# Triangle update and Fourier layer on one core: weights prepared on ScalarE in the gathering stage, rows spread by transfers, transposes ahead of the norm's factor, centering in two PSUM tiles

## The chip, the cores and the metric

The kernel runs on one core of one Trainium2 chip. The metric is device time in microseconds (us), the median of several executions. Lower is better. TensorE is written PE, VectorE DVE, ScalarE ACT, GpSimd POOL and SyncE SP; a DMA that SP or POOL issues stands in that engine's queue and starts when the engine's instruction stream reaches it.

## The reference, cut to what matters

The input `x` is 512 x 512 positions with 64 channels, float32. Layer 0 adds a triangle update, layer 1 adds a layer of 12 x 12 Fourier modes. Each is applied to a group norm over the whole image (32 groups of two channels).

```python
x = x + _L0_conv_ref(_gn(x), sequence_mask, norm_w, norm_b, left_w, left_b, ...)
x = x + _L1_conv_ref(_gn(x), w_real, w_imag)

def _L0_conv_ref(x, ...):
    xn = _ln(x, norm_w, norm_b)                      # over the 64 channels
    left  = (xn @ left_w  + left_b)  * mask * sigmoid(xn @ lgate_w + lgate_b)
    right = (xn @ right_w + right_b) * mask * sigmoid(xn @ rgate_w + rgate_b)
    out_gate = sigmoid(xn @ ogate_w + ogate_b)
    out = einsum('bkjd,bkid->bijd', left, right)
    return (_ln(out, onorm_w, onorm_b) @ out_w + out_b) * out_gate
```

`mask` is 1 only where row and column are both in the sequence mask (0 or 1 for each of the 512 rows), so the sides are needed only for masked rows and columns.

## The kernel before, in words

**The path.** The kernel ranks the masked rows first (lines 66 to 137) and, when there are at most K = 256 of them, takes the path `compact`, which this run takes. `slot_t` holds, row by row, the mask and the Fourier basis in rank order; `slot_row` holds each column's place among the masked ones.

**Stage 1, gathering (lines 682 to 725).** `load_weights` (line 685) issues 28 small loads on SP's queue: norm weights, the four weight matrices `raw_sides`, `raw_gates`, `raw_ogate`, `raw_out` and their biases. It returns `makers`, which later makes the steps that fold the norm into each weight: `begin` scales the raw matrix by the norm's weight on DVE (line 177) and multiplies by the centering matrix on PE (lines 179 and 180); `end` copies the result out of PSUM and adds the bias on DVE (lines 186 and 187). Then 16 blocks of 32 columns follow (`jc`, line 703). POOL gathers four tiles of 128 rows per block (line 644), 1 MB each: two with the masked rows (`xg`, two buffers of two tiles) and two with the others (`yg`). PE transposes each (line 713) into `x_ps` (six PSUM tiles), DVE takes the statistics from there (line 714). ACT copies 22 of the 32 columns of `xg` to their slots in `xc`, and POOL the other 10 (line 699, `keep`); since all of these write `xc` at places known only at run time, ACT's and POOL's copies take turns. After its copies POOL issues the gathers of block `jc + 2`. After the last block `group_norm_affine` (line 725) turns the statistics into `ab1`, the scale and shift of each channel: a chain of small DVE instructions with two PE averages (lines 261 to 290).

**Stage 2, sides and gates (lines 729 to 877).** `xc` is worked in 64 groups `q` of four columns. The order on each engine is the written one (`manual_schedule`), a software pipeline from q = -14 to 63 in which one pass of the loop does, for different groups:

- `project(q, "gates")` on PE, then the two sigmoids on ACT (line 839);
- `normed(q + 1)` on DVE (line 786), which reads `rbc`, the layer norm's factors spread over the channels;
- up to three of the nine steps of `rsqrt_steps` on DVE (`todo`);
- `channels(q + 14)`: four PE transposes into `xc_ps` (line 746, two tiles) and one ACT instruction that applies `ab1` (line 747);
- `spread(k)`, each fourth pass: a PE transpose into `rc_ps` (line 771), an ACT copy, then POOL writes the factors to DRAM (`rs_d`, line 775) and reads them back spread, twice 512 KB (`rbc`, line 779);
- one step of `making`, in passes -13 to -6 (line 849): the eight steps of the weights;
- `early`, six prefetches on POOL between q = 11 and 37;
- one step of `prepare`, in passes 51 to 60 (line 853);
- `centered(q + 13)`: four matmuls into the single tile `cc_ps` (line 754) and ACT's squares (line 758), which DVE sums (line 867);
- `project(q, "sides")` on PE, the product of side and gate on DVE (`o_c`, line 862), and two stores of 256 KB from SP's queue (`left_d`, `right_d`, line 874).

The factors of groups 4k to 4k + 3 are spread in pass 4k - 6, and `normed(4k)` runs in pass 4k - 1. `prepare` has ten steps: `mask_of` twice (lines 810 to 813: copy a mask column wide on DVE, transpose it on PE, copy it back on DVE) and `own_of` twice (lines 817 and 818), for the masks `mask_s` and `mask_own` of stage 3; `row_of` twice (lines 799 to 806), the biases of `ogate` and `out` as rows; `indices` twice (lines 822 to 824); and `center_x` and `gate_x` (lines 828 and 829).

**Stage 3 and after.** Stage 3 (from line 882) loads `left_d` and `right_d` channel by channel, multiplies them and applies the masks; its first load waits for the last store of stage 2. Then come output gate, second norm, Fourier layer and output, up to the end.

PSUM is full in stage 2: `xc_ps` two banks, `cc_ps` and `rc_ps` one each, `gates_c0`, `gates_c1`, `sides_c0`, `sides_c1` one each.

Of the kernel before, what the change touches and what calls it, by code (L numbers as in the profile page):

```python
# [46 lines left out]
def conv_preact_kernel(ctx: ExitStack, tc: tile.TileContext, t: dict):  # L47
# [94 lines left out]
    def load_weights(pool, queue):  # L142
# [27 lines left out]

        def steps(keep, room, slots=None):

            made = {}

            def begin(name, nw, nb, raw, b, k):
                scaled = pool.tile([P, P], F32, name="scaled_" + name, tag="scaled")
                nc.vector.tensor_scalar(scaled, raw, nw, None, ALU.mult)
                ps = made[name] = room()
                nc.tensor.matmul(ps[:, :P], center, scaled, start=True, stop=True)
                nc.tensor.matmul(ps[:, P : P + 1], raw[:k], nb[:k], start=True, stop=True)  # L180

            def end(name, nw, nb, raw, b, k):
                ps = made.pop(name)
                weights[name] = raw if slots and name in ("sides", "gates") else keep.tile([P, P], F32, name="w_" + name)
# [6 lines left out]
        return steps  # L191

# [57 lines left out]

    def group_norm_affine(keep, sets, each, name, with_mean=lambda: None, with_variance=lambda ab: None):

# [3 lines left out]
        ab = keep.tile([P, 3], F32, name="ab_" + name)  # L256
        with tc.tile_pool(name="gn_" + name, bufs=1) as gp, tc.tile_pool(
            name="gnp_" + name, bufs=1, space=PSUM
        ) as gps:
            part = gp.tile([P, groups], F32, name="part")  # L260
            nc.vector.tensor_reduce(part, sets[0], AX.X, ALU.add)
            mean_ps = gps.tile([P, groups], F32, name="mean_ps")
            nc.tensor.matmul(mean_ps, avg, part, start=True, stop=True)
# [10 lines left out]
            nc.vector.tensor_reduce(v, d, AX.X, ALU.add)  # L274
            var_ps = gps.tile([P, groups], F32, name="var_ps")
            nc.tensor.matmul(var_ps, avg, v, start=True, stop=True)
# [90 lines left out]
    def general(gc):  # L367
# [10 lines left out]
        with tc.tile_pool(name="wprep", bufs=1) as wp, tc.tile_pool(name="wps", bufs=2, space=PSUM) as wps:  # L378
            for step in load_weights(wp, nc.scalar)(gc, lambda: wps.tile([P, P + 1], F32, name="made_ps")):
                step()  # L380
# [246 lines left out]
    def compact(fc):  # L627
# [53 lines left out]
        with tc.tile_pool(name="wt", bufs=1) as cp:  # L681
            with tc.tile_pool(name="f1", bufs=1) as sp, tc.tile_pool(name="f1x", bufs=2) as xp, tc.tile_pool(
                name="f1y", bufs=4
            ) as yp, tc.tile_pool(name="f1p", bufs=6, space=PSUM) as pt, tc.manual_schedule():
                makers = load_weights(cp, nc.sync)
                sets = chunk_sets(fc, 4, 1)
# [16 lines left out]
                for jc in range(NJ):  # L703
                    if jc % quarter == 0:
                        stats = sp.tile([P, 1, 16 * quarter, 6], F32, name="stats1c")
                    for r in range(4):
                        flat = xgs[jc][1][r].rearrange("p j c -> p (j c)")
                        for c in range(4):

                            ps = pt.tile([P, 4, P], F32, name="x_ps")  # L710
                            for i in range(4):
                                o = (8 * c + 2 * i) * C
                                nc.tensor.transpose(ps[:, i, :], flat[:, o : o + P], ident)  # L713
                            nc.vector.bn_stats(  # L714
                                stats[:, 0, 16 * (jc % quarter) + 4 * r + c, :], ps.rearrange("p i k -> p (i k)")
                            )
                    keep(mybir.EngineType.Activation, nc.scalar.copy, jc, 0, SHARE)
                    keep(mybir.EngineType.Pool, nc.gpsimd.tensor_copy, jc, SHARE, JC)
                    del xgs[jc]
                    if jc + 2 < NJ:  # L720
                        fetch_tile(jc + 2)
                    if jc % quarter == quarter - 1:
                        join_chunks(sp, sets, jc // quarter, stats)

                ab1 = group_norm_affine(fc, sets, 2 * stats.shape[2], "xc")


            rs_d = dram.tile([K // 4, 2, 4 * P], F32, name="rs_d")
            with tc.tile_pool(name="fn", bufs=2) as np_, tc.tile_pool(name="fw", bufs=2) as wk, tc.tile_pool(
                name="fr", bufs=3  # L730
            ) as rp, tc.tile_pool(name="fg", bufs=1) as sp, tc.tile_pool(name="fo", bufs=5) as op, tc.tile_pool(
                name="fpt", bufs=2, space=PSUM
            ) as pt, tc.tile_pool(name="fpc", bufs=1, space=PSUM) as pc, tc.tile_pool(
                name="fpp", bufs=1, space=PSUM
            ) as pp, tc.manual_schedule():
                groups = K // 4
# [5 lines left out]

                def channels(q):
                    tps = pt.tile([P, 4, P], F32, name="xc_ps")
                    for i in range(4):
                        nc.tensor.transpose(tps[:, i, :], xc[:, 4 * q + i].rearrange("p r c -> p (r c)"), ident)
                    nc.scalar.activation(
                        gts(q), tps.rearrange("p i k -> p (i k)"), AF.Identity, bias=ab1[:, 1:2], scale=ab1[:, 0:1]
                    )

                def centered(q):
                    cps = pc.tile([P, 8, C], F32, name="cc_ps")
                    for i in range(4):
# [14 lines left out]
                def spread(k):  # L768

                    ps = pc.tile([QB * 8, P], F32, name="rc_ps")  # L770
                    nc.tensor.transpose(ps, rss.pop(k), ident)
# [23 lines left out]

                def row_of(name):

                    wide = sp.tile([P, P], F32, name="wide_" + name, tag="wide")
                    nc.vector.tensor_copy(wide, biases[name].to_broadcast([P, P]))
                    ps = pt.tile([P, 4, P], F32, name="xc_ps")[:, 0, :C]  # L800
                    nc.tensor.matmul(ps, wide, ident[:, :C], start=True, stop=True)
                    rows_of[name] = fc.tile([P, C], F32, name="bias_row_" + name)
                    nc.vector.tensor_copy(rows_of[name], ps)
                    if name == "out":
                        for r in range(2):
                            nc.sync.dma_start(u_d[:, K, r, :], rows_of["out"])

                def mask_of(b):
                    wide = sp.tile([P, P], F32, name=f"wide{b}", tag="wide")
                    nc.vector.tensor_copy(wide, slot_t[:, b, 1:2].to_broadcast([P, P]))  # L810
                    ps = pt.tile([P, 4, P], F32, name="xc_ps")[:, 0]
                    nc.tensor.matmul(ps, wide, ident, start=True, stop=True)
                    nc.vector.tensor_copy(mask_s[:, b * P : (b + 1) * P], ps)

                def own_of(b):
                    own = sp.tile([P, P], F32, name=f"own{b}", tag="wide")
                    nc.vector.tensor_mul(own, mask_s.rearrange("p (q b) -> p b q", b=2)[:, b], ident)
                    nc.vector.tensor_reduce(mask_own[:, b : b + 1], own, AX.X, ALU.add)

                def indices(b):  # L820
# [738 lines left out]
```

## Time and profile before

| | |
|---|---|
| timed, median of 3 | 1777.51 us (1775.67 to 1780.51) |
| the profiled execution | 1774.54 us |
| its span, first to last instruction | 1772.8 us |
| mean granted PE clock | 0.895 |
| stage 1 | 0 to 195 us |
| norm's factor, to the first ACT instruction of stage 2 | 195 to 201 us |
| stage 2 before the first `normed` | 201 to 232 us |
| stage 2, steady and end | 232 to 447 us |
| stage 3 | 450 to 613 us |

The profile has one row for each instruction or group of instructions: start, duration, engine, line, operation, what is written and read, and in square brackets how long the engine was idle just before and what ended that. `x4` is a count, and then the duration is that of the group. `PEld` is PE's load of the stationary operand. A table by stretches gives each engine's busy time in a window, the clock granted to PE (1.00 is full), the share of time in which the DMA engines were busy, and what they moved.

### The profile page before, as it was taken

What the parts mean: (1) busy time and instruction counts of PE and PEld (TensorE: products, weight loads), DVE (VectorE), ACT (ScalarE), POOL (GpSimd) and SP (SyncE); (2) the same over time, 40 slices, a digit from 0 to 9 for tenths busy, and PEclk for the clock granted to TensorE, in tenths of its full rate; (3) what the DMA queues carried; (4) which work ended last, traced back from release to release, by engine and by line L of the source; (5) the groups of instructions that cost most, each with busy time, mean ns of one, the idle gap of its engine ahead of it and who ended that gap; (6) DMA issues with size and microseconds to landing.
All of it is one profiled execution on the core that took longest, in us unless ns stands there. A gap on an engine that the chain in (4) does not pass through costs nothing. (4 is left out here: it accounts for less than half of the span.)

```text
span 1772.8 us, 32732 instructions
## 1 busy us (share of the span) xinstructions
PE 1559.8 (88%) x10918; PEld 1241.0 (70%) x10918; DVE 1411.4 (80%) x2985; ACT 946.9 (53%) x1724; POOL 935.4 (53%) x693
## 2 busy tenths in 40 slices
PE   6777699998899977999999999999999877998772
PEld 5666566664799866888888988888888744665441
DVE  6989678888455558889999999999999984865551
ACT  3555577774333356777777777777777642011000
POOL 4666111110000027799999999999999881111110
PEclk9999999999999989999999999999999975555555
DMA  7999268987899879568777767776777699999999
GB/s 284 386 380 382 109 174 276 288 276 237 278 309 306 273 217 342 221 203 308 246 257 260 243 237 250 261 254 233 257 264 243 208 305 418 422 426 427 427 427 382
DMA packets 192818, 518.48 MB, mean 292 GB/s; under 512 B 37920, under 2 KB 104736, under 8 KB 151680
## 3 DMA queue, kind: packets, MB, share of 16 engines
q1 hardware_dynamic: 156400, 295.72, 47.5%
q0 software_dynamic: 32768, 218.38, 33.6%
q10 hardware_dynamic: 3472, 2.20, 0.5%
q8 instruction: 88, 1.44, 0.3%
q14 instruction: 90, 0.74, 0.1%
HBM read 311.60 MB, written 204.60 MB: 291 GB/s over the span
## 5 line engine op out<-in xcount | busy, mean ns | idle before, releaser
L1070 PE MATMUL w_ps<-gate_x,xt_c 128*128 128x128 f32 x2048 | 281.1, 281 | 31.3 <-DVE z_t L1299 27.8
L1138 POOL TENSOR_TENSOR xc<-xc,z_t 128x1024 f32<-128x1024 f32 x127 | 301.2, 2372 | 8.1
L1070 PEld LDWEIGHTS w_ps<-gate_x,xt_c 128*128 128x128 f32 x2048 | 252.4, 194 | 48.4 <-DVE z_t L1299 44.2
L1070 PE MATMUL c_ps<-center_x,xt_c 128*128 128x128 f32 x2048 | 277.0, 279 | 1.3 <-ACT xt_c L1104 0.6
L1070 PEld LDWEIGHTS c_ps<-center_x,xt_c 128*128 128x128 f32 x2048 | 252.9, 194 | 4.2 <-ACT xt_c L1065 2.7
L1465 PE MATMUL l_ps<-xc,rinv 24*128 24x512 f32 x512 | 208.2, 1136 | 28.3 <-DVE xc L1472 18.6
L1193 DVE BATCH_NORM_STATS2 stats2c<-xc 128x6 f32<-128x128 f32 x1024 | 220.4, 278 | 8.9 <-POOL xc L1138 8.9
L1108 DVE TENSOR_REDUCE scratch<-sq_c 128x16 f32<-128x1024 f32 x160 | 194.5, 1216 | 24.1 <-ACT sq_c L1103 19.8
L1246 ACT ACTIVATE z_t<-z_t 128x1024 f32<-128x1024 f32 x128 | 135.5, 1059 | 132.8 <-DVE z_t L1305 110.7
L1303 POOL TENSOR_TENSOR z_t<-z_t,bias_row_out 128x1024 f32<-128x1024 f32 x32 | 75.5, 2360 | 245.6 <-DMA xc<-tri_d 223.0
L1465 PEld LDWEIGHTS l_ps<-xc,rinv 24*128 24x128 f32 x512 | 121.2, 306 | 110.5 <-DVE xc L1472 57.1
L1065 ACT ACTIVATE xt_c<-t_ps,ab_xc 128x512 f32<-128x512 f32 x256 | 176.1, 688 | 8.7 <-PE t_ps L1063 7.8
L1299 DVE TENSOR_TENSOR z_t<-w_ps,rs_n 128x512 f32<-128x512 f32 x256 | 172.1, 672 | 6.2 <-PE w_ps L1070 6.1
L714 DVE BATCH_NORM_STATS2 stats1c<-x_ps 128x6 f32<-128x512 f32 x256 | 155.5, 679 | 16.9 <-PE x_ps L713 16.0
L1101 ACT ACTIVATE sq_c<-c_ps 128x512 f32<-128x512 f32 x256 | 150.7, 589 | 31.1 <-PE c_ps L1070 30.6
L1305 DVE TENSOR_TENSOR z_t<-z_t,scratch 128x1024 f32<-128x1024 f32 x128 | 156.3, 1221 | 10.1 <-ACT rs_n L1114 3.5
L1134 POOL TENSOR_TENSOR z_t<-z_t,xc 128x1024 f32<-128x1024 f32 x64 | 151.8, 2371 | 15.7 <-ACT z_t L1246 15.6
L1063 PE MATMUL t_ps<-c_ident,xc 128*128 128x128 f32 x1024 | 157.9, 277 | 0.0
L1472 DVE TENSOR_TENSOR xc<-xc,l_ps 128x512 f32<-128x512 f32 x176 | 109.2, 682 | 56.6 <-DMA xc<-x_h,dst_i 44.4
L1063 PEld LDWEIGHTS t_ps<-c_ident,xc 128*128 128x128 f32 x1024 | 118.0, 142 | 50.9 <-issue 49.8
L1134 POOL TENSOR_TENSOR z_t<-z_t,bias_row_out 128x1024 f32<-128x1024 f32 x63 | 149.4, 2371 | 7.3 <-ACT z_t L1246 6.8
L699 ACT COPY xc<-xg 128x128 f32 x352 | 105.0, 298 | 67.6 <-POOL xc L699 28.7
(212 smaller groups left out, 2563.6 us busy)
## 6 DMA issues: line engine op xcount, KB each, us to landing
x_h<-xc SPq DMA_DIRECT2D x64, 1024.0 KB
out_x<-xc SPq DMA_DIRECT2D x44, 1024.0 KB
xc<-u_d SPq DMA_DIRECT2D x512, 64.0 KB
out_x<-lx_t SPq DMA_DIRECT2D x20, 1024.0 KB
rbc<-rs_d POOLq DMA_DIRECT2D x32, 512.0 KB, 7.0
left_d<-o_c SPq DMA_DIRECT2D x64, 256.0 KB
right_d<-o_c SPq DMA_DIRECT2D x64, 256.0 KB
left_raw<-left_d SPq DMA_DIRECT2D x64, 256.0 KB
```

What stands on the lines that cost most here:

```text
L714: nc.vector.bn_stats(stats[:, 0, 16 * (jc % quarter) + 4 * r + c, :], ps.rearrange("p i k -> p (i k)"))
L1063: nc.tensor.transpose(tps[:, i, :], flat[:, o : o + P], ident)
L1065: nc.scalar.activation(xts[s], tps, AF.Identity, bias=ab1[:, 2:3])
L1070: nc.tensor.matmul(ps[:, 2 * i : 2 * i + 2, :], xts[s][:, i, :], w, start=True, stop=True)
L1101: nc.scalar.activation(sq, cps, AF.Square)
L1108: nc.vector.tensor_reduce(totals[k % 2][:, 8 * (n - 1) : 8 * (n + 1)], sqs.pop(s // 2), AX.X, ALU.add)
L1134: nc.gpsimd.tensor_mul(zs[k, c], zs[k, c], u)
L1138: nc.gpsimd.tensor_add(xr, xr, zs.pop((k, c)))
L1193: nc.vector.bn_stats(st[k // 4][:, g, k % 4, :], x_of(k)[:, :, 2 * g : 2 * g + 2])
L1299: nc.vector.tensor_mul(z[:, 8 * odd : 8 * odd + 8, :], wps, rs)
L1305: nc.vector.tensor_add(z, z, bias_ps["ogate"].unsqueeze(1).to_broadcast([P, 16, C]))
L1465: nc.tensor.matmul(ps.rearrange("p j o -> p (j o)"), rinv[h, b, :], it[h], start=True, stop=True, tile_position=(32 * g, 0),)
```

## The change

The four weights are made in stage 1: ACT scales them before its copies of blocks 5 to 8 (`scale_weights`), PE centers them after the transposes of the same blocks (`center_weights`, into two PSUM tiles of their own, the bias added by a matmul with the identity), and ACT copies them out before its copies of block 10 (`keep_weights`). The masks and the two bias rows no longer go through DVE and PE: SP writes them to DRAM (`m_d`, `b_d`) and reads them back spread. The three mask transfers stand on SP's queue ahead of the weight loads; the bias rows follow `keep_weights`. `group_norm_affine` moves into stage 2's pools and calls `turn_x` for groups 0 to 5 between its second PE average and its `rsqrt`; groups 2 to 5 borrow the PSUM tiles of gates and sides. `centered` alternates, for groups below 13, between `cc_ps` and another tile (`rc_ps`, then tiles of gates and sides). What is left of `prepare` runs in passes 0 to 3 in place of 51 to 60.

```diff
+m_d = dram.tile([K], F32, name="m_d")
+nc.sync.dma_start(m_d.rearrange("(b p) -> p b", p=P), slot_t[:, : K // P, 1])
+nc.sync.dma_start(mask_s, m_d.unsqueeze(0).to_broadcast([P, K]))
+nc.sync.dma_start(mask_own, m_d.rearrange("(p b) -> p b", b=2))
-makers = load_weights(cp, nc.sync)
+loaded, _ = load_weights(cp, nc.sync)
+made = mk.tile([P, 4, P], F32, name="made_w")
+made_b = mk.tile([P, 4], F32, name="made_b")
+def scale_weights(i):
+    name, nw, nb, raw, b, k = loaded[i]
+    scales[i] = cp.tile([P, P], F32, name="scaled_" + name, tag="scaled")
+    nc.scalar.mul(scales[i], raw, nw)
+def center_weights(i):
+    name, nw, nb, raw, b, k = loaded[i]
+    nc.tensor.matmul(made[:, i, :], center, scales.pop(i), start=True, stop=True)
+    nc.tensor.matmul(made_b[:, i : i + 1], raw[:k], nb[:k], start=True, stop=False)
+    nc.tensor.matmul(made_b[:, i : i + 1], ident, b, start=False, stop=True)
+def keep_weights():
+    for i, (name, nw, nb, raw, b, k) in enumerate(loaded):
+        weights[name] = raw if i < 2 else fc.tile([P, P], F32, name="w_" + name)
+        nc.scalar.copy(weights[name], made[:, i, :])
+        biases[name] = b_all[:, i : i + 1]
+    nc.scalar.copy(b_all, made_b)
+    mkp.close()
+    b_d = dram.tile([2, C], F32, name="b_d")
+    for i, name in enumerate(("ogate", "out")):
+        nc.sync.dma_start(b_d[i].rearrange("(c o) -> c o", o=1), biases[name][:C])
+        rows_of[name] = fc.tile([P, C], F32, name="bias_row_" + name)
+        nc.sync.dma_start(rows_of[name], b_d[i].unsqueeze(0).to_broadcast([P, C]))
+    for r in range(2):
+        nc.sync.dma_start(u_d[:, K, r, :], rows_of["out"])
...
 for jc in range(NJ):
+    if 0 <= jc - 5 < 4:
+        scale_weights(jc - 5)
+    if jc == 10:
+        keep_weights()
...
+    if 0 <= jc - 5 < 4:
+        center_weights(jc - 5)
     keep(mybir.EngineType.Activation, nc.scalar.copy, jc, 0, SHARE)
...
-ab1 = group_norm_affine(fc, sets, 2 * stats.shape[2], "xc")
...
+four = ("gates_c0", "gates_c1", "sides_c0", "sides_c1")
+def turn_x(q):
+    if q < 2 or q > 5:
+        tps = pt.tile([P, 4, P], F32, name="xc_ps")
+    else:
+        tps = pp.tile([P, N], F32, name=four[q - 2]).rearrange("p (i k) -> p i k", i=4)
     for i in range(4):
         nc.tensor.transpose(tps[:, i, :], xc[:, 4 * q + i].rearrange("p r c -> p (r c)"), ident)
+    turned_x[q] = tps
 def channels(q):
-    tps = pt.tile([P, 4, P], F32, name="xc_ps")
+    if q not in turned_x:
+        turn_x(q)
+    tps = turned_x.pop(q)
...
 def centered(q):
-    cps = pc.tile([P, 8, C], F32, name="cc_ps")
+    if q % 2 == 0 or q >= lead:
+        cps = spare("cc_ps")
+    else:
+        cps = spare("rc_ps") if q < 7 else pp.tile([P, N], F32, name=four[(q - 7) // 2])
...
-prepare = [lambda b=b: mask_of(b) for b in range(2)] + [lambda b=b: own_of(b) for b in range(2)]
-prepare += [lambda: row_of("ogate"), lambda: row_of("out"), lambda: indices(0), lambda: indices(2)]
+prepare = [lambda: indices(0), lambda: indices(2)]
 prepare += [lambda: nc.vector.tensor_scalar(center_x, center, ab1[:, 0:1], None, ALU.mult)]
 prepare += [lambda: nc.vector.tensor_scalar(gate_x, weights["ogate"], ab1[:, 0:1], None, ALU.mult)]
-making = makers(fc, lambda: pp.tile([P, N], F32, name="gates_c0"), True)
+ab1 = group_norm_affine(
+    fc, sets, 2 * stats.shape[2], "xc", with_variance=lambda ab: [turn_x(q) for q in range(6)],
+    rooms=[lambda k=k: spare(k)[:, :1] for k in ("cc_ps", "rc_ps")],
+)
 for q in range(-lead - 1, groups):
...
-    if q + lead in range(1, 1 + len(making)):
-        making[q + lead - 1]()
...
-    if 0 <= q - (groups - lead) < len(prepare):
-        prepare[q - (groups - lead)]()
+    if 0 <= q < len(prepare):
+        prepare[q]()
```

`mask_of`, `own_of` and `row_of` are gone. Elsewhere the diff only passes these pieces through (`group_norm_affine` takes `rooms`, the pools of `cc_ps` and of the four tiles change places).

More of the change, by code (lines that the diff above doesn't have):

```diff
@@ L169, in load_weights, with steps @@
             loaded.append((name, *norms[norm], raw, b, C if split else P))
-        def steps(keep, room, slots=None):
+        def steps(keep, room):
             made = {}
@@ L183, in end @@
                 ps = made.pop(name)
-                weights[name] = raw if slots and name in ("sides", "gates") else keep.tile([P, P], F32, name="w_" + name)
+                weights[name] = keep.tile([P, P], F32, name="w_" + name)
                 biases[name] = keep.tile([P, 1], F32, name="b_" + name)
@@ L189, in steps @@
             return [lambda part=part, one=one: part(*one) for one in loaded for part in (begin, end)]
-        return steps
+        return loaded, steps
     def rsqrt(pool, total, scale, eps, shape, y=None):
@@ L249, in join_chunks, with group_norm_affine @@
         nc.vector.scalar_tensor_tensor(var, var, 1.0 / count, between, ALU.mult, ALU.add)
-    def group_norm_affine(keep, sets, each, name, with_mean=lambda: None, with_variance=lambda ab: None):
+    def group_norm_affine(keep, sets, each, name, with_mean=lambda: None, with_variance=lambda ab: None, rooms=None):
         groups, n = sets[0].shape[1:]
@@ L256, in group_norm_affine @@
         ab = keep.tile([P, 3], F32, name="ab_" + name)
-        with tc.tile_pool(name="gn_" + name, bufs=1) as gp, tc.tile_pool(
-            name="gnp_" + name, bufs=1, space=PSUM
-        ) as gps:
+        with tc.tile_pool(name="gn_" + name, bufs=1) as gp, ExitStack() as own:
+            if rooms is None:
+                gps = own.enter_context(tc.tile_pool(name="gnp_" + name, bufs=1, space=PSUM))
+                rooms = [lambda k=k: gps.tile([P, groups], F32, name=k + "_ps") for k in ("mean", "var")]
             part = gp.tile([P, groups], F32, name="part")
             nc.vector.tensor_reduce(part, sets[0], AX.X, ALU.add)
-            mean_ps = gps.tile([P, groups], F32, name="mean_ps")
+            mean_ps = rooms[0]()
             nc.tensor.matmul(mean_ps, avg, part, start=True, stop=True)
@@ L274, in group_norm_affine @@
             nc.vector.tensor_reduce(v, d, AX.X, ALU.add)
-            var_ps = gps.tile([P, groups], F32, name="var_ps")
+            var_ps = rooms[1]()
             nc.tensor.matmul(var_ps, avg, v, start=True, stop=True)
@@ L378, in general @@
         with tc.tile_pool(name="wprep", bufs=1) as wp, tc.tile_pool(name="wps", bufs=2, space=PSUM) as wps:
-            for step in load_weights(wp, nc.scalar)(gc, lambda: wps.tile([P, P + 1], F32, name="made_ps")):
+            for step in load_weights(wp, nc.scalar)[1](gc, lambda: wps.tile([P, P + 1], F32, name="made_ps")):
                 step()
@@ new lines, in compact @@
+                mkp = ExitStack()
+                mk = mkp.enter_context(tc.tile_pool(name="mk", bufs=1, space=PSUM))
+                made = mk.tile([P, 4, P], F32, name="made_w")
+                made_b = mk.tile([P, 4], F32, name="made_b")
+                b_all = fc.tile([P, 4], F32, name="b_all")
+                scales = {}
+                def scale_weights(i):
+                    name, nw, nb, raw, b, k = loaded[i]
+                    scales[i] = cp.tile([P, P], F32, name="scaled_" + name, tag="scaled")
+                    nc.scalar.mul(scales[i], raw, nw)
@@ L732, in compact @@
                 name="fpt", bufs=2, space=PSUM
-            ) as pt, tc.tile_pool(name="fpc", bufs=1, space=PSUM) as pc, tc.tile_pool(
-                name="fpp", bufs=1, space=PSUM
-            ) as pp, tc.manual_schedule():
+            ) as pt, tc.tile_pool(name="fpp", bufs=1, space=PSUM) as pp, tc.tile_pool(
+                name="fpc", bufs=1, space=PSUM
+            ) as pc, tc.manual_schedule():
                 groups = K // 4
@@ L741, in gts, with spare, channels @@
                     return xc[:, 4 * q : 4 * q + 4].rearrange("p i r c -> p (i r c)")
-                def channels(q):
-                    tps = pt.tile([P, 4, P], F32, name="xc_ps")
+                four = ("gates_c0", "gates_c1", "sides_c0", "sides_c1")
+                turned_x = {}
+                def turn_x(q):
[3 more added lines that the diff above has]
+                        tps = pp.tile([P, N], F32, name=four[q - 2]).rearrange("p (i k) -> p i k", i=4)
                     for i in range(4):
                         nc.tensor.transpose(tps[:, i, :], xc[:, 4 * q + i].rearrange("p r c -> p (r c)"), ident)
+                    turned_x[q] = tps
+                def spare(name):
+                    return pc.tile([P, N], F32, name=name)
+                def channels(q):
+                    if q not in turned_x:
+                        turn_x(q)
+                    tps = turned_x.pop(q)
                     nc.scalar.activation(
@@ L751, in centered @@
                 def centered(q):
-                    cps = pc.tile([P, 8, C], F32, name="cc_ps")
+                    if q % 2 == 0 or q >= lead:
+                        cps = spare("cc_ps")
+                    else:
+                        cps = spare("rc_ps") if q < 7 else pp.tile([P, N], F32, name=four[(q - 7) // 2])
+                    cps = cps.rearrange("p (i c) -> p i c", c=C)
                     for i in range(4):
@@ L768, in spread @@
                 def spread(k):
-                    ps = pc.tile([QB * 8, P], F32, name="rc_ps")
+                    ps = spare("rc_ps")[: QB * 8, :P]
                     nc.tensor.transpose(ps, rss.pop(k), ident)
@@ L793, in project @@
                     return made
[L796 to L818, printed above, removed]
                 def indices(b):
```

## The prediction

> **What bounds the kernel now.** I read the page's 40 slices first (the clock and DMA rows dip near 200 us and near 410 us), then the table by stretches around both dips, then the timeline inside them, then the waits. Columns of the table: PE, PEld, DVE, ACT and POOL busy, granted PE clock, DMA share, GB/s.
>
> ```profile
> 198.20:201.90 3.70, 2.40 (x11) 2.00 (x11) 1.79 (x12) 0.83 (x2) 0.00 (x0) 0.50 0.02 4
> 201.90:205.70 3.80, 2.94 (x13) 2.54 (x13) 0.88 (x2) 1.99 (x3) 0.00 (x0) 0.59 0.00 0
> 205.70:220.00 14.30, 10.66 (x79) 9.20 (x80) 5.49 (x18) 6.34 (x10) 0.00 (x0) 1.00 0.00 0
> 250.00:400.00 150.00, 150.00 (x891) 91.60 (x887) 129.64 (x273) 110.89 (x187) 26.35 (x39) 1.00 0.89 274
> 404.00:448.00 44.00, 34.81 (x133) 16.46 (x130) 34.98 (x75) 19.53 (x32) 3.50 (x6) 0.96 0.81 246
> ```
>
> From 250 to 400 us PE is busy all the time and the DMA share is 0.89: one pass takes 3.40 us (`o_c` starts at 247.04 and 250.45) and nothing is to be had there. Before 220 us no engine is full and the DMA engines are idle; from 404 us on PE and DVE are both at 79%. These are chains, and the change touches both. The first one, in the timeline:
>
> ```profile
> 204.07 0.60 ACT L758 ACTIVATE sqc<-cc_ps 128x512 f32<-128x512 f32 x1 [1.56 <-PE cc_ps L754]
> ...
> 207.61 0.60 ACT L758 ACTIVATE sqc<-cc_ps 128x512 f32<-128x512 f32 x1 [1.97 <-PE cc_ps L754]
> ...
> 208.26 0.97 PEld L754 LDWEIGHTS cc_ps<-c_center,xc 128*128 128x128 f32 x8 [0.49 <-ACT sqc L758]
> ...
> 209.46 0.60 ACT L758 ACTIVATE sqc<-cc_ps 128x512 f32<-128x512 f32 x1 [0.58 <-PE cc_ps L754]
> ...
> 216.91 0.30 PEld L179 LDWEIGHTS gates_c<-scaled_ogate,c_center 128*128 128x128 f32 x2 [1.96 <-DVE scaled_ogate L177]
> ...
> 221.56 0.24 ACT L773 COPY turned_c<-rc_ps 32x128 f32<-32x128 f32 x1
> ...
> 232.23 0.68 DVE L786 TENSOR_TENSOR xnc<-xc,rbc 128x512 f32<-128x512 f32 x1
> ```
>
> The squares start at 204.07, 207.61, 209.46, 212.95, 214.80, 218.56, 220.40, 223.61, 225.46 and then every 1.85 us. Passes with a `begin` are long, because PE stands behind DVE's `scaled` (third fence line from the end); passes without one take 1.85 us, because the one `cc_ps` must be read (0.49 us wait) before the next centering. The whole stage 2 hangs on the first factors, copied at 221.56 and used at 232.23. The other end:
>
> ```profile
> 407.55 1.41 DVE L862 SCALAR_TENSOR_TENSOR o_c<-sides_c,b_sides,sigc 128x512 f32<-128x512 f32 x2 [0.41 <-ACT sqc L758]
> ...
> 410.87 0.49 PE L812 MATMUL xc_ps<-c_ident,wide 128*128 128x128 f32 x2 [2.46 <-DVE wide L810]
> ...
> 412.50 1.41 DVE L862 SCALAR_TENSOR_TENSOR o_c<-sides_c,b_sides,sigc 128x512 f32<-128x512 f32 x2 [0.82 <-DMA right_d<-o_c]
> ```
>
> PE waits 2.46 us for `wide`, since its transpose stands ahead of the sides in PE's order, and the pass takes 4.95 us. From 437.01 on, with little or no `prepare`, the passes take 2.10 us (445.40 for the last).
>
> **The change, part by part.** All terms are against the profiled execution, 1774.54 us.
>
> *Weights out of the passes -13 to -6.* The four long periods exceed 1.85 by 1.69, 1.64, 1.91 and 1.36: **-6.6 us**, of which 5.2 fall before the copy at 221.56.
>
> *Two tiles for centering.* The trace shows no pass without the wait on `cc_ps`, so I bound the pace: above by today's 1.85, below by PE's own work, 0.47 for four transposes and 0.88 for a centering (PEld 228.84, and 227.96 to 228.84), 1.35. ACT needs 1.18 (starts 0.50 and 0.68 apart), DVE 0.6 plus three steps of 0.2. I take 1.35, because all three rows fit in it. Six periods stand between the first squares and the copy: 3.0 us. The copy comes at 221.56 - 5.2 - 3.0 = 213.3. Then DMA is late next: the second `rbc` issue began at 224.97, 3.41 after the copy, and `rbc` lands 5.4 to 7.4 us after issue (the tile's answer: 5.4/7.0/7.4). So 213.3 + 3.41 + 5.4 to 7.4 is 222.1 to 224.1; I take 223.1, against 232.23. That is 9.1 in all, so **-2.5 us** beyond the weights.
>
> *Six groups transposed ahead.* Today the two groups that PE transposes there take 1.95 us (198.69), at clock 0.50; later four transposes take 0.47. The 24 now stand ahead of the first centering in PE's order. At the slow rate they take 5.85 us, to 204.5, at the fast one 2.8; the centering today ends at 203.98 and then would end between 202.8 (`channels(0)` is done at 201.83) and 205.6. I take **0**, -1.2 to +1.6. The Trainium skill ("TensorE: Matmul & The Clock Gate", Part 1) says that PE runs at half rate until a free-running window of about 3.4 us has been busy; this speaks against putting more work there. By it some 14 transposes would be slow and the centering would end near 204.1; the trace agrees as far as the clock is 0.50, then 0.59, then 1.00.
>
> *What follows the first factors.* ACT's table load (1.28 us) ended 0.66 us after the gates did; ACT now waits for `rbc` and loads meanwhile: **-0.6**. But PE, done with its centerings near 220, now idles some 3.5 us before the first gates. After its idle 193.36 to 196.82 the clock was 0.50 and 0.59 for 6.8 us. Here the pass is PE's, so that would cost up to 3.4 us, or nothing; I take **+1.5**.
>
> *`prepare` in passes 0 to 3.* DVE gets 0.52, 0.36, 0.28 and 0.28 us. It waits about 0.4 a pass for squares or sides (13.0 and 5.4 us in 45 waits), which covers all but a little: **+0.3**, 0 to 1.4 without that cover.
>
> *`prepare` out of passes 51 to 60.* From `o_c` at 407.55 to that at 445.40 are 13 passes, 37.85 us. Without it: 13 x 2.10, three passes with 0.6 of `rsqrt` steps and one last sum of 0.6, 29.7: **-8.1 us**. Late next is `rbc` of the last four groups. From its copy (422.41) to the end of its issue (427.77) and to landing are up to 12.1 us; the normalization that needs it would come 0.35 + 4 x 2.10 + 1.4 = 10.2 us after the copy: a wait of 1.9. DMA is also fuller: 13 x 0.52 MB of stores and 2.1 MB of `rbc` in 29.7 us are 300 GB/s, where the loop above reaches 274 at a share of 0.89. I take **+2.5**, 0 to 5.
>
> *Stage 1.* ACT's four scalings and five copies cost 0.30 each (line 699, 128x128). They stand before its copies of a block, where ACT idles 3.8 us on average (28.7 + 27.8 us in 15 waits for POOL or DMA): hidden; 2.6 us if reading the slots into registers fills that idle time. PE's six small matmuls take 1.25 us a block (0.49, 0.38, 0.38 at 205.69) and PE idles 0.7 to 1.9 us there: hidden, or 2 us. DMA, which is full in this stage, gets some 900 small packets; SP's queue moved 3200 in the first 60 us in 5.1% of the 16 engines' time, 15 ns each, so 0.9 us. The SP queue now does the masks first: `m_d` can start at 14.2 (`slot_t`), lands 1.4 (`rs_d`) to 15 us (the slowest gather) later, then come 28 loads at 1.48 us (their spacing from 24.33 to 36.18), of which the sides' are through by the 14th: landed by 65, before ACT wants them at 72.7. Nothing else is on SP's queue until 238. Sum **+0.8**, 0 to 5. A page of the skill ("DMA: Bandwidth & Descriptors", rules for kernel authors) says that a non-contiguous last dimension makes one descriptor per element; by it `m_d` is 256 descriptors, which are in the 900.
>
> Sum: -6.6 - 2.5 - 0.6 + 1.5 + 0.3 - 8.1 + 2.5 + 0.8 = **-12.7 us**. The profiled execution lies 3.0 below the median, so 1761.8 becomes 1764.8 for a median: **1765 us**. Stage 3's first load waits for stage 2's last store (450.07), and everything later follows from stage 3, so I carry the gain to the end whole.
>
> **The rivals.**
> 1. *Transfers take the place of the waits.* The chain ends on `rbc` twice, and in the end DMA may be the bound. For it: share 0.89 in the loop. Against it: 0.81 at the end, and no landing over 7.4. With the worst of both (5 us at the end, 224.1 and a cold PE, 3.4) the gain is 12.7 - 2.5 - 1.0 - 1.9 = 7.3: 1770.
> 2. *All of it arrives.* No wait at the end, landing in 5.4, clock kept: gain 12.7 + 2.5 + 1.0 + 1.5 + 0.8 + 0.3 = 18.8: 1759.
> 3. *The change does not shorten the path*: 1.85 stays the pace (2.5 lost) and stage 1 pays for what it takes on (5 of 0.8), with rival 1: 7.3 - 2.5 - 4.2 = 0.6: 1777.
> 4. *Slower.* In stage 1 ACT's and POOL's copies take turns with next to no slack (ACT 7.25 us, POOL 3.48, period 10.9), and POOL's gathers stand behind its copies. If ACT at block 5 waits for `raw_sides` behind SP's mask transfers, each us goes into the span. It must eat 12.7 + 5.3 = 18 us, so the load must land after 95, and SP's loads would need 3.6 us each in place of 1.48. At 4.3 us each the 14th lands at 104: 1764.8 + 27 = 1792 us. Against it: the fixed spacing in the trace.
>
> **How the numbers follow.** A measurement of this kernel tells a change from none at about 0.3%, 5.3 us. Chances: forecast (1760 to 1767) 0.55, rival 1 (1767 to 1772) 0.20, rival 2 0.10, rival 3 0.08, rival 4 0.07. Faster 0.85, same 0.08, slower 0.07. The range reaches from rival 2's side of the sum, with the start at its earliest (1757), to the worst of rival 1 with half of stage 1's bound (1773), and leaves out rivals 3 and 4.
>
> **What would show it.** Right: squares about 1.35 us apart between 205 and 220 us, a first `xnc` near 223 that waits for DMA `rbc`, `o_c` every 3.40 us after it, 2.1 us apart at the end with one wait for DMA near the 60th, stage 1 ending within 1 us of 195. Wrong: ACT waiting for a weight or for PE ahead of block 5 or 10, squares still 1.85 apart, `o_c` 2.5 us or more apart at the end, or PE's clock below 1.00 for long after 223.

## The result and the profile after

The changed kernel takes 1782.26 us (median of 12 executions, 1774.54 to 1788.51) against 1776.36 (12 executions of the kernel before, 1774.14 to 1780.51). The ratio is 1.0033, with a 95% interval of 1.0018 to 1.0048: slower by about 6 us, where 1765 was forecast. The profiled execution took 1782.45 us with a span of 1780.7, so it is 7.9 us longer than the profiled one before.

The span is cut at the same marks in three profiles: when the norm's factor `ab` is complete, the first squares, the first `turned_c` copy, the first `xnc`, the first `o_c`, the `o_c` of pass 50, the last `o_c`, and the end. The fourth column is the experiment with contiguous writes, told below. All in us.

| stretch | before | after | contiguous writes | forecast change | change after |
|---|---|---|---|---|---|
| start to `ab` | 200.95 | 215.06 | 199.60 | +0.8 | **+14.1** |
| `ab` to the first squares | 3.12 | 5.25 | 3.21 | 0 | +2.1 |
| squares to the copy | 17.49 | 8.85 | 8.84 | -8.2 | -8.6 |
| copy to the first `xnc` | 10.67 | 10.51 | 10.43 | -0.9 | -0.2 |
| `xnc` to the first `o_c` | 4.51 | 7.29 | 4.52 | +0.9 | +2.8 |
| 50 passes | 170.81 | 171.70 | 172.05 | +0.3 | +0.9 |
| last 13 passes | 37.85 | 37.56 | 36.36 | -5.6 | **-0.3** |
| last `o_c` to the end | 1327.4 | 1324.5 | 1327.2 | 0 | -2.9 |

From the first squares to the first `xnc` stage 2 came as forecast (-8.8 us against -9.1), but the stretch on either side of that lost about 2 us more than forecast; stage 1 lost 14 us, and the end gave its gain back. The table by stretches of after, with the columns of the one before (granted clock, DMA share and GB/s are the last three):

```profile
215.06:220.31 5.25, 5.25 (x32) 5.25 (x31) 0.00 (x0) 1.55 (x2) 0.00 (x0) 0.62 0.00 0
220.31:229.16 8.85, 7.85 (x65) 7.07 (x64) 6.17 (x16) 8.53 (x15) 0.00 (x0) 1.00 0.00 0
239.67:246.96 7.29, 6.54 (x22) 3.98 (x24) 3.28 (x12) 2.53 (x4) 1.24 (x2) 0.54 0.66 145
418.66:456.22 37.56, 32.04 (x105) 15.04 (x102) 27.54 (x49) 16.61 (x27) 3.10 (x6) 0.91 0.80 232
250.00:400.00 150.00, 149.37 (x884) 90.82 (x881) 129.36 (x276) 109.85 (x185) 25.69 (x39) 1.00 0.88 267
```

In the squares' stretch ACT is now busy 8.53 of 8.85 us: it has become the bound there. The steady loop is unchanged. The clock is low in the first and third row.

**Stage 1.** First SP's queue, then ACT's copies of whole blocks in `xc`, and the same copies in the kernel before:

```profile
132.46 0.47 SPq L721 DMA_DIRECT2D b_d<-b_all  x1
144.11 0.33 SPq L723 DMA_DIRECT2D bias_row_ogate<-b_d  x1
144.49 0.74 SPq L721 DMA_DIRECT2D b_d<-b_all  x1
160.78 0.33 SPq L723 DMA_DIRECT2D bias_row_out<-b_d  x1
```
```profile
135.29 7.23 ACT L740 COPY xc<-xg 128x128 f32 x22 [2.85 <-POOL xc L740]
152.62 7.27 ACT L740 COPY xc<-xg 128x128 f32 x22 [10.10 <-DMA xg<-in_x,src_i]
170.21 7.23 ACT L740 COPY xc<-xg 128x128 f32 x22 [10.31 <-DMA xg<-in_x,src_i]
```
```profile
131.83 7.24 ACT L699 COPY xc<-xg 128x128 f32 x22 [3.58 <-POOL xc L699]
143.35 7.26 ACT L699 COPY xc<-xg 128x128 f32 x22 [4.28 <-DMA xg<-in_x,src_i]
154.36 7.25 ACT L699 COPY xc<-xg 128x128 f32 x22 [3.75 <-DMA xg<-in_x,src_i]
```

A write of 64 bias values is issued at 132.46, and the read that waits for it goes out at 144.11; the second pair takes 16.3 us. Meanwhile the blocks start 17.3 and 17.6 us apart, where before and in the blocks ahead of these it is 10.8 to 11.8: ACT waits 10 us for a gather, twice. What the DMA engines moved from 125 to 165 us, in 40 slices of 1 us, says why:

```profile
GB/s 434 393 336 369 336 221 426 393 410 426 442 402 410 98 25 49 82 82 49 57 33 172 385 443 408 398 421 411 418 57 33 74 131 139 139 49 25 107 385 418
```

For eight slices, and again for nine, some 25 to 140 GB/s pass instead of 400. The gathers are in flight meanwhile: from 138 to 146 us the DMA engines count as busy 0.92 of the time, with 71 packets of the gathers, about 1.7 us each, where the 684 from 125 to 138 us took about 0.33 us each. The first write of the change, `m_d`, is issued at 10.75 and its read at 21.99; the first block's copies start at 25.38, before at 21.67. From 17 to 23 us, most of which SP waits for this write, 86 GB/s pass; in the kernel with contiguous writes it is 404.

**The two waits for `rbc`**, at the start and at the end of stage 2:

```profile
229.16 0.24 ACT L836 COPY turned_c<-rc_ps 32x128 f32<-32x128 f32 x1
...
239.67 0.69 DVE L849 TENSOR_TENSOR xnc<-xc,rbc 128x512 f32<-128x512 f32 x1 [2.68 <-DMA rbc<-rs_d]
...
240.41 2.08 PE L855 MATMUL gates_c<-xnc,raw_gates 64*128 64x512 f32 x4 [3.44 <-DVE xnc L849]
...
428.99 0.24 ACT L836 COPY turned_c<-rc_ps 32x128 f32<-32x128 f32 x1
...
434.35 1.23 POOL L842 DMA_DIRECT2D rbc<-rs_d  x2 [4.31 <-DVE o_c L901]
...
444.60 0.69 DVE L849 TENSOR_TENSOR xnc<-xc,rbc 128x512 f32<-128x512 f32 x1 [5.65 <-DMA rbc<-rs_d]
```

From the last copy to the use of its `rbc` are 15.6 us; the passes it crosses now take 2.0 to 2.6 each, so DVE waits 5.65 us. At both places PE then works slowly: four gate matmuls take 2.08 us (240.41), in passes before the last wait 1.29 (426.49).

### The profile page after: what moved, and what is told of

Same layout as the page of the kernel before. It is cut to its first block, busy times and chain, and to the rows that moved or that the text cites. A ratio compares the mean times of both kernels' runs of the same rounds, so it can differ in the third digit from the quotient of the medians.

```text
span 1780.7 us, 32739 instructions
## 1 busy us (share of the span) xinstructions
PE 1557.7 (87%) x10918; PEld 1247.9 (70%) x10918; DVE 1410.2 (79%) x2961; ACT 947.6 (53%) x1733; POOL 935.4 (53%) x693
## 5 line engine op out<-in xcount | busy, mean ns | idle before, releaser
L1147 DVE TENSOR_REDUCE scratch<-sq_c 128x16 f32<-128x1024 f32 x160 | 194.6, 1216 | 22.8 <-DMA xc<-tri_d 10.9
```

The source lines that it names most:

```text
L1147: nc.vector.tensor_reduce(totals[k % 2][:, 8 * (n - 1) : 8 * (n + 1)], sqs.pop(s // 2), AX.X, ALU.add)
```

## The experiments

The theory (T1) is that the writes of 4-byte pieces to DRAM hold up the gathers in stage 1. The rivals: the weights' work on ACT and PE breaks the turns of the copies (T2); the way through DRAM, or the reads that spread a row, cost the time (T3). Each ratio is to executions of the kernel before from the same session (medians 1775.55 to 1777.94); after itself was timed with the result alone, so a difference to its 1782.26 is one across sessions.

**Without any of the transfers.** `mask_of`, `own_of` and `row_of` are put back into passes 51 to 56.

```diff
-nc.sync.dma_start(m_d.rearrange("(b p) -> p b", p=P), slot_t[:, : K // P, 1])
...
-nc.sync.dma_start(b_d[i].rearrange("(c o) -> c o", o=1), biases[name][:C])
...
+late = [lambda b=b: mask_of(b) for b in range(2)] + [lambda b=b: own_of(b) for b in range(2)]
+late += [lambda: row_of("ogate"), lambda: row_of("out")]
```

> After, but masks and bias rows are made on PE and DVE in passes 51 to 56 as before; no small transfer is left. Theory T1 (the writes of 4-byte elements to DRAM hold up the gathers): stage 1 is back, the norm's `ab` is ready at 200 to 202 us (before 200.95, after 215.06), no gather lands later than 10 us, and the time is 3 to 8 us under before. Rival T2 (ScalarE's and TensorE's work on the weights breaks the turns of the copies): `ab` stays at 213 to 216 and the time at 1780 to 1783.

Measured: 1767.84 us, ratio to before 0.9955 (0.9940 to 0.9971), 8 us less. `ab` is ready at 201.29, and the blocks are about 10.9 us apart, with two of 12.2 and 12.7 and none of 17. The slowest gather into `xg` still landed after 14.1 us (before 15.0, after 22.3), so the bound of 10 us was set too tight. T2 falls: the weights' work is all still there. The last 13 passes take 37.74 us with a wait for `rbc` of 0.25: the row steps make passes of 3.77 us, and these cover the transfer. So removing them, with the last spread where it was, could not have brought 8 us.

**One kind of transfer at a time.** The same edit, for the rows alone (masks stay transfers) and for the masks alone.

> After, with the masks by transfers and the bias rows made as before. T1: only the first write stays, and stage 1 is 3.7 us longer than before's, `ab` at 204 to 205. T2: `ab` at 213 to 216, as the weights are still made in stage 1. A third theory, that the later 11 us come from keep_weights' five copies alone, gives the same 213 to 216.

> After, with the bias rows by transfers and the masks made as before. T1: the two writes at block 10 stay, two blocks of some 17 us instead of 10.9, `ab` at 210 to 214; the first block's copies start at 21.7 as before. T2: 213 to 216, with long blocks that do not stand at the writes.

Masks by transfer: 1775.08 us, ratio 1.0001 (0.9983 to 1.0018), `ab` at 202.98; the first block starts at 24.74 instead of 21.9, but 1.7 to 2.0 us are left of it at the end, less than expected; the theory of the five copies falls too. That its time is no better than before's lies at the end: its last 13 passes take 41.56 us, with a wait for `rbc` of 5.58, since the two row steps come before the passes that the last transfer crosses and no longer cover it. Rows by transfer: 1779.45 us, ratio 1.0019 (1.0001 to 1.0037), `ab` at 210.33, with blocks 16.0 and 15.3 us apart exactly at the two writes. The two small writes of 64 values are the larger part of what stage 1 lost.

**The same transfers, written in one piece.** PE turns the column into a row on one partition, ACT copies it, and SP writes that.

```diff
-nc.sync.dma_start(b_d[i].rearrange("(c o) -> c o", o=1), biases[name][:C])
+nc.tensor.matmul(made[0:1, i, :C], b_all[:, 2 + i : 3 + i], ident[:, :C], start=True, stop=True)
+nc.scalar.copy(b_row, made[0:1, :2, :C])
+nc.sync.dma_start(b_d[i : i + 1], b_row[:, i])
```

(the rows one block later; `m_d` in the same way from `m_row`)

> After with the same transfers, but what goes to DRAM is first turned on PE into one row on one partition, so that the writes are one piece of 1 KB and two of 256 bytes in place of 256 and 2 x 64 pieces of 4 bytes; the reads that spread them are unchanged. T1 (the 4-byte pieces): stage 1 is as before within 1.5 us, `ab` at 200 to 203, time 4 to 9 us under after. Rival T3 (the way through DRAM, or the reads that spread a row over 128 partitions): the long blocks stay, `ab` at 211 to 216.

Measured: 1764.24 us, ratio 0.9939 (0.9913 to 0.9966), 11 us under before, and 18 under after where 4 to 9 were expected. `ab` is at 199.60: of the 18.5 us between the two profiles, 15.5 lie ahead of it. T3 falls: the way through DRAM and the spreading reads are the same and cost nothing at the end of the stage.

**The write by itself.** Three kernels are the kernel before with one write added at block 10, which nobody reads. Each was executed once.

```diff
+t_s = cp.tile([P, P], F32, name="t_s")
+nc.scalar.copy(t_s, ident)
+nc.sync.dma_start(t_d.rearrange("(c o) -> c o", o=1), t_s[:C, 0:1])   # adjacent: t_d is [C]
+nc.sync.dma_start(t_d[:, 0:1], t_s[:C, 0:1])                          # spaced: t_d is [C, P]
+nc.sync.dma_start(t_d, t_s[:C])                                       # rows: t_d is [C, P]
```

(one of the last three lines in each)

> Before, with one thing added: at block 10 ScalarE copies a 128x128 tile and SP writes 64 elements of 4 bytes of it, one from each partition, side by side to DRAM; nobody reads them. T1 (the write itself holds up the gathers): the block in which it is in flight takes some 17 us instead of 10.9, `ab` at 206 to 208 in place of 200.95. Rival T3 (it takes the read that follows the write, or what else the change does in stage 1): under 1 us.

> As the run before it, but the 64 elements of 4 bytes go to DRAM 512 bytes apart. If what costs is that many small pieces go to the same few lines of DRAM: under 2 us. If each small piece costs by itself: `ab` at 206 to 208 as with adjacent ones.

> As the run before it, with whole rows of 512 bytes in place of the 4 bytes: 64 pieces again, to the same addresses, 32 KB. If the number of pieces costs: `ab` at 206 to 208. If their size below some hundred bytes costs: under 1 us, for the 32 KB are 0.1 us at the 353 GB/s of this stage.

`ab` is ready at 207.31 with adjacent pieces, 201.05 with spaced ones and 198.97 with rows, against 200.95 before; the block with the adjacent pieces takes 15.8 us, where some 17 was expected. The times are 8.8 us above, 2.1 above and 2.5 below the kernel before. What was moved from 125 to 165 us, in slices of 1 us, with adjacent pieces, then spaced ones, then rows:

```profile
GB/s 336 401 360 369 385 393 410 410 426 434 197 49 90 57 66 57 57 74 393 426 410 401 442 418 410 451 426 410 418 410 451 426 393 410 426 442 377 344 426 418
```
```profile
GB/s 360 254 385 369 410 426 434 418 418 352 385 344 246 336 352 401 410 451 410 418 385 434 377 295 369 336 401 410 426 434 418 328 369 336 262 303 344 393 426 418
```
```profile
GB/s 377 401 426 426 426 410 423 420 336 360 360 320 360 410 393 434 426 426 369 401 369 320 311 328 369 401 426 426 442 352 377 360 320 352 385 401 385 418 442 434
```

The first row has seven slices of 49 to 90 GB/s; the others have none. So in one profile each, 64 pieces of 4 bytes cost 6.4 us when they lie side by side, and 0.1 us when the same 64 pieces lie 512 bytes apart. In the eight profiles without adjacent pieces `ab` comes between 198.97 and 201.36, so the 6.4 is clear of that spread and the 0.1 is nothing that can be told. It is neither the number of pieces nor their size alone. One such write is enough for a long block.

The Trainium skill ("DMA: Bandwidth & Descriptors", Specifications) says that a transfer under 512 bytes is done as a read-modify-write. If that alone were the price, both kinds of 4-byte pieces should be dear; the run with spaced pieces, whose `ab` is 0.1 us later than before, shows none of that. That adjacent pieces wait for each other where they fall into the same 512 bytes would fit both, but was not shown.

**An early last spread.** In the kernel after, the last group's factors are finished in pass 51 and spread at its end, into a third buffer.

```diff
-rbs[k] = np_.tile([P, QB, N], F32, name="rbc")
+rbs[k] = np_.tile([P, QB, N], F32, name="rbc", bufs=3)
-for step in todo[:3]:
+n = len(todo) if q == groups - lead else 3
+for step in todo[:n]:
...
+if q == groups - lead:
+    spread(groups // QB - 1)
```

> After, with the last group's factors finished in pass 51 in place of 51 to 53, their spread issued at the end of pass 51 in place of pass 54, and a third buffer for `rbc`, so that this write need not wait for a reader. Theory T4 (the tail's gain was given back to the last `rbc`, which has to be asked for while passes take 2.1 us): the pass of 7.67 us goes, the last 13 passes take 30 to 32 us (after 37.56), the time is 5 to 8 us under after's 1782. Rival (the DMA engines are the bound of these passes, whatever the order): `rbc` lands later or the stores hold up `o_c`, the 13 passes still take 35 us or more.

Measured: 1775.65 us, ratio 1.0000 (0.9987 to 1.0014), 6.6 us under after's median. The last 13 passes take 30.61 us:

```profile
419.65 0.26 ACT L836 COPY turned_c<-rc_ps 32x128 f32<-32x128 f32 x1 [2.75 <-PE rc_ps L834]
...
426.50 1.24 POOL L842 DMA_DIRECT2D rbc<-rs_d  x2 [5.79 <-DVE xnc L849]
...
436.20 0.69 DVE L849 TENSOR_TENSOR xnc<-xc,rbc 128x512 f32<-128x512 f32 x1 [0.58 <-DMA rbc<-rs_d]
```

The copy to its use now takes 16.5 us (after: 15.6), but the wait is 0.58. The DMA engines moved 286 GB/s in the passes around it (408.0 to 445.32), where after moves 232 in its last 13 passes, so they could: lateness was the cause, and the rival, that DMA is full there, falls.

**PE kept busy.** In the kernel after, 24 transposes into a tile that nobody reads stand behind the last centering ahead of the first gates.

```diff
+if q == -1:
+    warm = pp.tile([P, N], F32, name="gates_c1")
+    for i in range(24):
+        nc.tensor.transpose(warm[:, :P], center, ident)
```

> After, with 24 transposes that nobody reads on PE while it waits for the first `rbc`, so that it idles under 1 us there in place of 3.6. If the lower clock after that idle time is what costs: the granted clock stays at 1.00 from 235 to 250 us, the first normalization is followed by the first `o_c` 4.5 us later in place of 7.29, and the time is 2 to 3 us under after. Rival (the first pass waits for ScalarE's table load and sigmoids): 7.3 us as in after, no gain.

Measured: 1777.79 us, ratio 1.0004 (0.9991 to 1.0017); the medians differ by 4.5 us, and the profiles by 2.8 at this place. From the first `xnc` to the first `o_c`, this kernel:

```profile
236.83:241.36 4.53, 3.85 (x23) 2.35 (x24) 3.28 (x12) 4.30 (x6) 1.24 (x2) 1.00 0.63 150
```

4.53 us at clock 1.00, where after has 7.29 at 0.54: the price of the idle time is the clock. That the transposes kept the clock is not shown by this run alone: the kernels with contiguous writes and with the early spread, which idle there as after does, also kept it and took 4.52 and 4.53 us. In every kernel of this study the stretch takes 4.50 to 4.53 us with the full clock, and 6.08 to 7.43 where it fell.

**All three together.**

> The contiguous writes, the early last spread and the 24 transposes together. If the three losses are separate: stage 1 as before (`ab` at 200 to 201), 27 us from there to the first `o_c`, 30 to 32 us for the last 13 passes, and 1756 to 1760 us, some 17 us under before. Rival (the loop's DMA load takes the tail's gain): 1763 to 1766 as with contiguous writes alone.

Measured: 1760.08 us, ratio 0.9902 (0.9879 to 0.9925), at the upper end of what was expected. `ab` at 201.37, 26.9 us to the first `o_c`, 31.32 for the last 13 passes. It beats both kernels: 15.6 us under before, 22 under after.

**Two parts undone**, in the kernel with contiguous writes: every centering in `cc_ps`, and no transposes ahead of the norm's factor.

```diff
-if q % 2 == 0 or q >= lead:
-    cps = spare("cc_ps")
-else:
...
+cps = spare("cc_ps")
```
```diff
-with_variance=lambda ab: [turn_x(q) for q in range(6)],
```

> The kernel with contiguous writes (its stage 1 is undisturbed), with every centering in `cc_ps` as before. If the two tiles gave what the prediction priced: squares 1.85 us apart in place of 1.33 or less, from the first squares to the copy 11.9 us in place of 8.84, so about 3 us more, some 1767. Rival (ACT's and PE's order alone sets the pace once the weights are gone): no difference.

> The kernel with contiguous writes, with groups transposed one by one in their passes and none ahead of the norm's factor by hand. If transposing ahead only moves PE's work: the first squares come up to 1 us earlier after `ab` (3.2 us in the kernel with it), the first passes are PE's at 1.35 us each, and the copy comes within 1 us of 12.05 us after `ab`. Rival (the 24 transposes warm PE's clock and spare the passes): the copy 2 us or more later.

One tile: squares 1.85 us apart, each centering again waiting for the squares,

```profile
206.23 0.60 ACT L831 ACTIVATE sqc<-cc_ps 128x512 f32<-128x512 f32 x1 [0.58 <-PE cc_ps L827]
...
206.88 1.16 PE L827 MATMUL cc_ps<-c_center,xc 128*128 128x128 f32 x8 [0.69 <-ACT sqc L831]
```

and 12.23 us from the first squares to the copy instead of 8.84. The second tile is worth 3.4 us there. None ahead: the squares start 3.12 us after `ab` (3.21 with them), but the second is 2.23 later, and the copy comes 13.15 us after `ab` instead of 12.05: 1.1 us, where 0 was taken and up to 1 expected. That transposing ahead is worth these 1.1 is not shown: from `ab` to the copy, kernels that have it and two tiles took 11.91 to 14.09 us, mostly depending on when PE's clock came back to 1.00 (0.87 to 3.96 us after `ab`, and 4.89 in the kernel with none ahead). The times, 1768.22 (ratio 0.9941, 0.9921 to 0.9961) and 1766.24 (0.9934, 0.9916 to 0.9952), don't separate either from the kernel they were taken from (0.9939): the intervals are wider than these parts. What the second tile is worth is read from one profile, in which all six periods up to the copy are 1.84 or 1.85 us.

## Why the prediction was wrong

- **The step that failed is stage 1**: "DMA, which is full in this stage, gets some 900 small packets; SP's queue moved 3200 in the first 60 us in 5.1% of the 16 engines' time, 15 ns each, so 0.9 us." That rate was read from loads and applied to writes, and it prices only the time of the packets themselves. That time was small, as forecast; what the term put at nothing is what adjacent 4-byte writes do to the packets of the gathers, 1.7 us each instead of 0.33. (The sum of 0.8 is also less than the one term in it that is not hidden, 0.9.) Stage 1 measured +14.1 us, of which all but a fraction goes with the transfers (201.29 without them) and all of it when they are written in one piece (199.60). The upper bound of 5 us was built from the rest of the stage's terms and had no term for a write that slows others down; the nearest row for a small write, `rs_d`, is of rows of 512 bytes, and the 1.4 us that POOL waits for it (224.35 in the profile before) said nothing of smaller pieces. The waits of ACT that were feared, for a weight or for PE, did not come: block 10 found its weights made, and the copies of the weights lay in idle time.
- **The last 13 passes**: the mechanism, `rbc` late in passes of 2.1 us, was named, but "I take +2.5" should have been +7.8 (-0.3 came of the -8.1). The wait was priced at 1.9 us from an `rbc` that lands up to 12.1 us after its copy. In after it is used 15.6 us after the copy: the issue ends 6.6 us after it instead of 5.4, the landing takes up to 9.5 us where 7.4 was the longest before, and the wait is 5.65. After it, with PE's clock at 0.50, the next pass is 4.07 us long. Rival 1 had this mechanism and bounded it by 5.
- **The clock after the first wait**: "I take +1.5", bound 3.4; with ACT's table load (-0.6) the stretch was put at +0.9, and it took +2.8. With the clock kept at 1.00 it took 4.52 or 4.53 us, the same as before, so the -0.6 did not show and the +2.8 is the clock's.
- **The transposes ahead**: 0 was taken, +2.1 measured. In the other kernels with this part the stretch took 3.07 to 4.17 us, and its length goes with PE's mean granted clock in it: 3.07 at 0.86 (early spread), 3.21 at 0.81 (contiguous writes), 4.17 at 0.63 (rows only). In after it is 5.25 at 0.62, and there the transposes also start 1.3 us later: POOL's last copies, which they need, ended at 214.06, only 1.0 us before `ab`. So of the 2.1, by an estimate from these rows, about 1.1 to 1.3 are the late copies and the rest is the clock. The prediction had the clock as its range (5.85 us for the 24 transposes at the slow rate, 2.8 at the fast one), with an end of +1.6, but no late copies.
- **Right**: the weights out of the passes and the two tiles (-8.2 forecast, -8.6); the squares' pace of 1.35 up to the copy (1.16 to 1.36; PE's own work did not bound it, since ACT is busy 8.53 of the 8.85 us); the first `xnc` limited by `rbc`; a loop of 3.40 us (3.43).
- **The sum**: with the three losses removed the span is 1760.2 us, 12.6 less than before's 1772.8. The forecast was -12.7. That the two agree is partly luck, since the terms do not match one by one: the tail there gives 6.5 instead of 5.6, and the 50 passes cost 2.4 instead of 0.3. The 50 passes took 170.8 to 174.5 us in the profiles of this study, for reasons that are not known. Nor is it known why after gained 2.9 us behind the last `o_c`: that stretch took 1324.5 to 1328.6 us, and 1327.2 with contiguous writes.

Rival 4, the one that ended on the slower side, had the right place (stage 1, the gathers) and a wrong mechanism: the weight loads were in time.

What stays open: why adjacent pieces are so dear, from which spacing on they are not (only 4 and 512 bytes were tried), and why the 256 adjacent values of `m_d` leave only 2 us at the end of the stage, less than 64 in the middle of it. They too hold the gathers up: with the masks alone by transfer 116 GB/s pass from 17 to 23 us, and the first block starts 4.1 us later than with contiguous writes. Part of that is made up in the blocks that follow; how was not shown.

## What to carry to other kernels

Don't spread a column by writing it to DRAM with one small piece for each partition while other transfers matter: turn it into a row on chip first, and write that in one piece. A rate read from loads is no price for stores; where no row shows the kind of transfer that is added, put what it may do to the others into the range. When passes become faster, look at every transfer that was asked for a fixed number of passes ahead: its lead shrinks with them.

## What the hardware showed

- 64 adjacent 4-byte pieces bring the DMA engines from about 400 to 49 to 90 GB/s for seven slices of 1 us. At block 10, 11.7 us pass from the issue of the first such write to the read that waits for it; with 256 bytes in one piece, 4.1 us (138.15 to 142.28). Around the second of these single-piece writes three slices are left with 148 to 251 GB/s, and no block is longer for it by more than 1.5 us; the read that spreads the first row is in flight there too, so these slices can't be put down to the write.
- At the first gates PE's granted clock falls to 0.50 after idle times of 3.38, 3.44, 3.57, 3.72 and 3.85 us (rows only; after; none ahead; masks only; no transfers), and stays at 1.00 after 3.36 and 3.38 (contiguous writes; early spread). The low clock costs 1.6 to 2.9 us there. The length of the idle time does not decide it: in the kernel before, 1.98 us of it (413.28 to 415.26) were enough, and the clock is 0.50 from 416.67 to 420.08. In the profiles the clock changes only at points of a grid of 3.41 us, such as 212.19, 219.01, 239.49 and 246.32 us in after (2, 6 and 2 steps apart), and what divides the seven cases is how much of the idle time falls between two such points: 2.0 to 2.7 us where the clock fell, at most 1.8 where it stayed. So a shift of the same idle time by a microsecond can decide it. The Trainium skill ("TensorE: Matmul & The Clock Gate", Part 1) describes a free-running window of about 3.4 us; the grid agrees with it.
